# A cross-network kernel on one core: seven half-width matmuls in place of eight per 2x2 block of outputs

## The chip, the core and the metric

The kernel runs on one core of a Trainium2 chip. The metric is the device time of one launch in microseconds (us), the median of several runs. The core has a matrix engine (PE in the profile, PEld for its weight loads), a vector engine (DVE), a scalar engine (ACT), GpSimd (POOL) and a queue engine (SP) that issues most transfers. Matrix products accumulate in PSUM, which holds eight banks of 128 x 512 numbers; everything else lies in SBUF. All numbers are 32-bit floats.

## The reference

1024 rows, each with 64 features of 16 elements, go through three layers that multiply features pairwise; the rest is sums.

```
for i in range(3):                                   # W0, W1, W2
    z = einsum('bfe,bge->bfge', x0, h).reshape(B, f0 * fh, e)
    y = einsum('oc,bce->boe', W[i], z) + b[i][None, :, None]
    x_i, h = (y[:, :64], y[:, 64:]) if i < 2 else (y, y)
    xs.append(x_i)
pooled = sum(concatenate(xs, axis=1), axis=2)
return pooled @ fc_w.T + fc_b
```

## The kernel before

**What is computed.** The last layer is only ever summed with fixed weights, so the kernel folds W2, W1 and the final weights into one matrix at the start (the "set-up", up to some 46 us). After that each row needs two sets of 64 numbers, both linear in the products x_f * x_g of the row with itself: "h" (the kept half of layer one) and "q" (its partner). The result is the sum of (h + bias) * q, plus a small linear and quadratic part.

**Tiles.** The 1024 rows are 32 chunks of 32 rows, so a chunk is 512 columns (32 rows x 16 elements). The distinct products of a chunk are 16 tiles of 128 x 512; tile t = 4j + i. One `product` (line 234) makes the four tiles of one j: the operand `xa` (128 x 4 x 512) times the operand `xb` of that j (128 x 512). `contract` (line 256) sends the 16 tiles of a chunk through PE: 128 weight columns (64 of h, 64 of q, in `w_all`) against 512 columns, added up in one bank. Each such matmul stands as two rows in the trace, each with its weight load.

**Chunks.** Four chunks at the head (2, 3, 0, 1 in `HEAD`) get h alone first, by `half_contract` (line 297), because the q weights are not ready; q follows in `head_q` (line 315): 64 weight columns, one chunk in the upper and the other in the lower half of the array. The other 28 chunks go through `contract` whole. The squares and linear parts that the tiles leave over are `contract_shared` (lines 272, 277, 285): 24 matmuls of 32 rows x 64 columns for every four chunks.

**After PE.** For each chunk ACT copies the q half out of PSUM (line 331), DVE multiplies it with h (`factors`, line 337), and for each pair of chunks `x_v0x` (342) and `sums` (346) finish the row sums.

**Order.** The order is written out by hand: the list `order` and the loop behind it fix what each engine does next, and each engine works in that order, waiting for its inputs and for a free buffer. `load_products` loads a chunk's `xa` and `xb` on SP (1 MiB each) and has DVE make its 16 tiles; 12 buffers hold products, three each hold `xa` and `xb`. GpSimd makes only three groups of products, all at the head.

Of the kernel before, what the change touches and what calls it, by code (L numbers as in the profile page):

```python
# [42 lines left out]
F = 64  # L43
E = 16
# [15 lines left out]
FIRST = 4  # L60
SQ = slice(96, 128)


@with_exitstack
def cin_kernel(ctx, tc, xra, xrb, wh, w0r, w1h, w2t, wx1, wx0, vec, out):
# [3 lines left out]
    setup = ctx.enter_context(tc.tile_pool(name="setup", bufs=1))  # L69
    xp = ctx.enter_context(tc.tile_pool(name="xp", bufs=3))  # L70
    zp = ctx.enter_context(tc.tile_pool(name="zp", bufs=12))
# [8 lines left out]
    def z_tile(name):  # L80

        return zp.tile([128, NI, N], F32, tag="z", name=name)

    def flat_tile(name):
        return z_tile(name).rearrange("p i n -> p (i n)")

    def set_tile(name):
        return setup.tile([128, NI * N], F32, tag="set", name=name)
# [9 lines left out]
    nc.scalar.copy(fv2, fc2.to_broadcast([128, 32]))  # L98

    v0w = const_tile("v0w", [128, 2, F])  # L100
    v1w = const_tile("v1w", [128, 2, F])

    misc = ps.tile([128, N], F32, tag="acc", name="misc", bufs=4)

# [20 lines left out]
    w_all = const_tile("w_all", [128, NT, 192])  # L125
    w_sq = const_tile("w_sq", [128, 192])

    res = const_tile("res", [128, 128])


    xas, xbs, xxs, xrs, sqs = {}, {}, {}, {}, {}
# [12 lines left out]
    def load_xb(c, first=NJ):  # L144

        xb = xp.tile([128, NJ, N], F32, tag="xb", name=f"xb_{c}")
        for at in (slice(0, first), slice(first, NJ)):
            if at.start < NJ:
                nc.sync.dma_start(out=xb[:, at, :], in_=xrb[c, :, at, :])
        xbs[c] = [xb[:, j, :] for j in range(NJ)]  # L150

    def load_shared(first):

        xr = xrs[first] = sp.tile([128, 2, N], F32, tag="xr", name=f"xr_{first}")
        for k in (first // 2, first // 2 + 1):
            xxs[k] = sp.tile([128, N], F32, tag="xx", name=f"xx_{k}", bufs=4)
        for n in range(4):
            c = first + n
            nc.sync.dma_start(
                out=xr[32 * n : 32 * n + 32],  # L160
                in_=bass.AP(
                    tensor=xra.tensor, offset=c * XR * N, ap=[[N, 32], [32 * N, 2], [1, N]]
                ),
            )
            nc.sync.dma_start(out=xxs[c // 2][halves[c % 2]], in_=xra[c, 0:F])
        sqs[first] = sp.tile([128, N], F32, tag="sq", name=f"sq_{first}")
        nc.scalar.activation(sqs[first], xr[:, 0, :], AF.Square)  # L167
# [6 lines left out]
    w0t = z_tile("w0t")  # L174
    w2s = [flat_tile(f"w2_{k}") for k in range(2)]
    w1s = set_tile("w1s")
# [8 lines left out]
    xb_gps = xp.tile([128, NJ, N], F32, tag="xb", name="xb_gps")  # L185
# [4 lines left out]
    load_xb(c2, 1)  # L190
# [23 lines left out]

    acc = const_tile("acc", [128, 2, NCH // 2, CB])
    hb = const_tile("hb", [128, NF // 2, N])
    accs, uus, zs, ys, parts = {}, {}, {}, {}, {}
# [12 lines left out]
    def product(c, j, first=0, last=NI, engine=nc.vector):  # L230
        if first == 0:
            zs[c, j] = z_tile(f"z_{c}_{j}")
        at = slice(first, last)
        engine.tensor_tensor(  # L234
            zs[c, j][:, at, :], xas[c][:, at, :],
            xbs[c][j].unsqueeze(1).to_broadcast([128, last - first, N]), ALU.mult,
        )
        if j == NJ - 1:
            nc.scalar.activation(zs[c, j][SQ, 0, :], xas[c][SQ, 0, :], AF.Square)  # L239

    def w_cols(c):
        return slice(64, 192) if c % 2 else slice(0, 128)

    def tiles(j):

        return (1, 2, 3, 0) if j == NJ - 1 else range(NI)
# [5 lines left out]
    def contract(c, j, piece=0):  # L252
        acc_c, cols = pieces(c)[piece]
        for i in tiles(j):
            t = j * NI + i
            nc.tensor.matmul(  # L256
                acc_c, w_all[:, t, w_cols(c)], zs[c, j][:, i, cols],
                start=(t == 0 and c % 4 < 2), stop=(t == NT - NI and c % 4 >= 2),
            )

    def contract_shared(first):

        chunks = range(first, first + 4)
        ends = chunks if first == 0 else chunks[:2]
        for k in (first // 2, first // 2 + 1):
            ys[k] = ps.tile([128, N], F32, tag="y", name=f"y_{k}")
        groups = {c: slice(32 * (c % 4), 32 * (c % 4) + 32) for c in chunks}
        for m in range(2):
            for c, at in groups.items():
                n, xr = c % 2, xrs[first][groups[c], m]  # L270
                for acc_c, cols in pieces(c):
                    nc.tensor.matmul(  # L272
                        acc_c[halves[1 - n]], v1w[at, m], xr[:, cols],
                        start=(m == 0 and c not in ends), stop=False,
                        tile_position=(at.start, 64 * (1 - n)),
                    )
                nc.tensor.matmul(  # L277
                    ys[c // 2][halves[n]], v0w[at, m], xr, start=(m == 0), stop=(m == 1),
                    tile_position=(at.start, 64 * n),
                )  # L280
        for c, at in groups.items():
            for acc_c, cols in pieces(c):
                for n in range(2):
                    h = n == c % 2
                    nc.tensor.matmul(  # L285
                        acc_c[halves[n]], w_sq[at, w_cols(c)][:, 64 * n : 64 * n + 64],
                        sqs[first][at, cols], start=h and (first == 0 or c not in ends),
                        stop=(c in ends), tile_position=(at.start, 64 * n),
                    )


    def half_contract(c, *js, last=None):
        for j in js:
            for i in tiles(j):
                t = j * NI + i
                for n in range(2):
                    nc.tensor.matmul(  # L297
                        accs[c][halves[n]], w_all[:, t, 0:64],
                        zs[c, j][:, i, n * H2 : (n + 1) * H2],
                        start=(t == 0), stop=(j == last and i == tiles(j)[-1]),  # L300
                    )

# [8 lines left out]
    def head_q(k, j):  # L311
        for i in tiles(j):
            t = j * NI + i
            for c in (2 * k, 2 * k + 1):
                nc.tensor.matmul(  # L315
                    accs[c][halves[1 - c % 2]], w_all[:, t, 64:128], zs[c, j][:, i, :],
                    start=(t == 0), stop=False,
                )

    def uu_tile(k):  # L320
        if k not in uus:
            uus[k] = sp.tile([128, 2, N], F32, tag="uu", name=f"uu_{k}")
        return uus[k]

    def factors(c, which=slice(0, 1)):

        uu = uu_tile(c // 2)[halves[c % 2], 0, :]
        h = halves[c % 2]
        for acc_c, cols in pieces(c)[which]:
            q = sp.tile([128, N], F32, tag="q", name=f"q_{c}_{cols.start}")  # L330
            nc.scalar.copy(q[h, cols], acc_c[64 - h.start : 128 - h.start])  # L331
            if c in HEAD:
                hc = hb[h, c // 2, :]
                nc.vector.tensor_tensor(hc, acc_c[h], hc, ALU.add)
                nc.vector.tensor_tensor(uu, hc, q[h], ALU.mult)
                continue
            nc.vector.scalar_tensor_tensor(  # L337
                uu[:, cols], acc_c[h], bh1[h], q[h, cols], ALU.add, ALU.mult
            )

    def x_v0x(k):
        nc.vector.scalar_tensor_tensor(uu_tile(k)[:, 1, :], ys[k], cx, xxs[k], ALU.add, ALU.mult)  # L342

    def sums(k, rows=slice(0, 128), of=slice(0, 2), half=slice(0, CB)):
# [3 lines left out]
            uus[k][rows, of, E * half.start : E * half.stop].rearrange("p k (b e) -> p k b e", e=E),  # L348
# [17 lines left out]
    nc.scalar.copy(xb_gps[:, 0, :], xbs[c0][1])  # L366
    xbs[c0][1] = xb_gps[:, 0, :]
# [11 lines left out]
    nc.vector.memset(w0o[3][SQ, 0, :], 0.0)  # L379
    for j in (2, 3):  # L380
        h1_weights(j, w0o[j])
    half_contract(c0, 0)
# [8 lines left out]
    nc.scalar.copy(xb_gps[:, 1, :], xbs[c1][3])  # L391
    xbs[c1][3] = xb_gps[:, 1, :]
# [12 lines left out]
    v2r = flat_tile("v2r")[:, 0:1024].rearrange("p (n c) -> p n c", n=2)  # L405
    v2t = res[:, 0:F]
    for n in range(2):
# [7 lines left out]
        nc.vector.transpose(v2r[:, n, :], pv)  # L415


    v2q = v2r.rearrange("p n (s r) -> p (n s) r", r=32)[:, :, 0]
    for h in range(2):
        at = slice(32 * h, 32 * h + 32)  # L420
        nc.vector.tensor_copy(v2t[halves[h], at], v2q[halves[h]])
        nc.scalar.copy(v2t[halves[1 - h], at], v2q[halves[h]])
    half_contract(c1, 0, 3, 1)


    m_sb = z_tile("m_sb")
# [4 lines left out]
    for m in (0, 1):  # L431
        for n in range(2):
            for h in range(2):
# [3 lines left out]
                )  # L437

# [32 lines left out]
    )  # L471

# [4 lines left out]
    nc.scalar.copy(cx, pcx)  # L477
# [4 lines left out]
    for j in range(NJ):  # L482
        product(c2, j)
    product(c3, NJ - 1, engine=nc.gpsimd)
# [3 lines left out]
    ms = set_tile("ms").rearrange("p (v t g) -> p v t g", v=2, g=F)  # L488
# [30 lines left out]
    for j in range(NJ - 1):  # L519
        product(c3, j)  # L520
# [6 lines left out]
    dg = res[:, F:128]  # L527
    nc.sync.dma_start(out=dg[SQ], in_=m_ap(32, 32, [[row + F, 32], [1, F]]))
    nc.sync.dma_start(out=w_sq[:, 64:128], in_=m_ap(0, 0, [[0, 4], [row + F, 32], [1, F]]))
# [7 lines left out]

# [258 lines left out]
```

## Time and profile before

| | |
|---|---|
| time of three runs | 484.93, 485.12, 485.13 us; median 485.12 us |
| span of the profiled execution | 483.0 us, 4429 instructions |
| around the span, against the median | 2.1 us |
| line 256 (128 weight columns), PE | 387.6 us busy, 928 rows |
| line 315 (64 weight columns), PE | 27.9 us busy, 128 rows |
| line 234, DVE | 278.3 us busy, 124 groups of four tiles, 2285 ns each |
| transfers | 87.01 MB, mean 180 GB/s |
| clock of PE | 1.000 of full speed throughout |

The page prints the span of the one profiled execution and not its time; its own time is taken as the span and the 2.1 us around it. In the rows, "out<-in" names the tile written and the tiles read, then partitions x elements; "x64" counts rows; a bracket at the end tells how long the engine stood idle before and what ended that. Busy times of neighbouring instructions overlap by their ends, so the distance between two starts is the better price of an instruction in a row of equals.

### The profile page before, as it was taken

To read this page: it belongs to the slowest core of one execution; us is meant where nothing else is said; L and a number is where in the kernel's file an instruction comes from. 1 tells how busy PE (TensorE), PEld (TensorE's weight loads), DVE (VectorE), ACT (ScalarE), POOL (GpSimd) and SP (SyncE) were. 2 spreads that over 40 slices of the span, in tenths; PEclk is the share of its full clock that TensorE was granted. 3 is DMA by queue.
4 is the path that set the end of the run, shared out by engine and by line. 5 is a ranking of instruction groups with operands and counts; after the bars stand their busy time and mean duration, and the time that the engine had idled before them with its cause. 6 is when DMAs were issued, how large, how long until landed. Compare 5 with 4: busy or idle time off the path is not lost.

```text
span 483.0 us, 4429 instructions
## 1 busy us (share of the span) xinstructions
PE 478.9 (99%) x1808; PEld 215.6 (45%) x1808; DVE 368.6 (76%) x227; ACT 67.5 (14%) x143; POOL 15.4 (3%) x17
## 2 busy tenths in 40 slices
PE   8999999999999999999999999999999999999997
PEld 4564344443344444444444444444444444444555
DVE  4993699998899988898887686766878677771321
ACT  3242033011110111001100010001000010000001
POOL 5330000000000000000000000000000000000000
PEclk9999999999999999999999999999999999999999
DMA  8986997662962683487247344373346631000000
GB/s 328 415 271 178 386 364 296 216 219 101 341 241 102 221 280 120 176 280 279 110 169 210 159 174 175 151 214 105 139 174 210 224 125 51 0 1 0 0 1 1
DMA packets 19660, 87.01 MB, mean 180 GB/s; under 512 B 4820, under 2 KB 5492, under 8 KB 10744
## 3 DMA queue, kind: packets, MB, share of 16 engines
q1 hardware_dynamic: 18584, 85.71, 49.8%
q10 hardware_dynamic: 1056, 1.02, 0.9%
q8 instruction: 14, 0.23, 0.2%
q14 instruction: 6, 0.05, 0.0%
HBM read 85.08 MB, written 1.64 MB: 180 GB/s over the span
## 4 chain that ended last, share of the span: by engine, by line
PE 98%; DMA 1%; DVE 1%; issue 0%; ACT 0%
PE acc L256 80%; PE acc L315 6%; PE acc L297 6%; PE acc L272 3%; PE acc L285 1%; PE xp L204 1%; DMA xa<-in_xra 1%; DVE z L234 1%; PE pm L434 0%; PE pv L410 0%; PE y L277 0%; PE pl L715 0%; DVE uu L337 0%; PE pc L651 0%; PE po L612 0%
## 5 line engine op out<-in xcount | busy, mean ns | idle before, releaser
L256 PE MATMUL acc<-z,w_all 128*128 128x512 f32 (+2 forms) x928 | 387.6, 579 | 0.0
L234 DVE TENSOR_TENSOR z<-xa,xb 128x2048 f32<-128x2048 f32 x124 | 278.3, 2285 | 41.4 <-PE acc L256 35.1
L256 PEld LDWEIGHTS acc<-z,w_all 128*128 128x128 f32 x928 | 173.1, 190 | 213.0 <-issue 205.9
L239 ACT ACTIVATE z<-xa 32x512 f32<-32x512 f32 x34 | 21.3, 626 | 336.9 <-DVE z L234 334.9
L337 DVE SCALAR_TENSOR_TENSOR uu<-acc,vs,q 64x512 f32<-64x512 f32 (+2 forms) x29 | 21.2, 731 | 58.0 <-ACT q L331 57.8
L297 PE MATMUL acc<-z,w_all 128*64 128x256 f32 x256 | 28.9, 381 | 0.4 <-DVE z L234 0.4
L315 PE MATMUL acc<-z,w_all 128*64 128x512 f32 x128 | 27.9, 593 | 0.0
L331 ACT COPY q<-acc 64x512 f32<-64x512 f32 (+2 forms) x33 | 18.7, 566 | 35.9 <-PE acc L256 19.8
L297 PEld LDWEIGHTS acc<-z,w_all 128*64 128x64 f32 x256 | 17.8, 137 | 12.7 <-DVE z L234 2.0
L234 DVE TENSOR_TENSOR z<-xa,xp 128x2048 f32<-128x2048 f32 (+2 forms) x12 | 20.3, 1747 | 0.7 <-PE xp L204 0.7
L346 DVE TENSOR_REDUCE acc<-uu 128x64 f32<-128x1024 f32 (+3 forms) x18 | 20.0, 1117 | 0.3
L315 PEld LDWEIGHTS acc<-z,w_all 128*64 128x64 f32 x128 | 9.1, 137 | 18.0 <-issue 16.8
L277 PE MATMUL y<-xr,v0w 32*64 32x512 f32 x128 | 15.9, 600 | 0.0
L272 PE MATMUL acc<-xr,v1w 32*64 32x512 f32 (+2 forms) x132 | 15.7, 587 | 0.0
L342 DVE SCALAR_TENSOR_TENSOR uu<-y,cx,xx 128x512 f32<-128x512 f32 x16 | 11.3, 747 | 0.2
L272 PEld LDWEIGHTS acc<-xr,v1w 32*64 32x64 f32 x132 | 5.1, 131 | 10.0 <-issue 9.0
L234 POOL TENSOR_TENSOR z<-xa,xb_gps 128x512 f32<-128x512 f32 (+2 forms) x4 | 9.4, 2373 | 4.8 <-ACT xb_gps L366 4.8
L285 PE MATMUL acc<-sq,w_sq 32*64 32x512 f32 (+2 forms) x132 | 8.7, 574 | 0.0
L533 DVE TENSOR_TENSOR w_all<-ms 128x256 f32<-128x256 f32 x4 | 1.5, 424 | 5.4 <-DMA ms<-md 5.4
L167 ACT ACTIVATE sq<-xr 128x512 f32<-128x512 f32 x8 | 5.0, 630 | 3.3 <-DMA xr<-in_xra 3.1
L204 PE MATMUL xp<-xa,shift 64*64 64x512 f32 x32 | 5.2, 754 | 0.3 <-DMA xa<-in_xra 0.3
L285 PEld LDWEIGHTS acc<-sq,w_sq 32*64 32x64 f32 x132 | 3.7, 132 | 3.7 <-issue 3.5
(66 smaller groups left out, 69.5 us busy)
## 6 DMA issues: line engine op xcount, KB each, us to landing
xa<-in_xra SPq DMA_DIRECT2D x32, 1024.0 KB
xb<-in_xrb SPq DMA_DIRECT2D x31, 1024.0 KB, 7.1
xr<-in_xra SPq DMA_DIRECT2D x32, 128.0 KB, 13.7
xx<-in_xra SPq DMA_DIRECT2D x32, 128.0 KB, 7.7
w<-in_w2t SPq DMA_DIRECT2D x2, 1024.0 KB, 12.0
w1s<-in_w1h SPq DMA_DIRECT2D x1, 1024.0 KB
w1x<-in_wx SPq DMA_DIRECT2D x1, 1024.0 KB
w0x<-in_wx SPq DMA_DIRECT2D x1, 1024.0 KB, 6.0
```

The costliest lines, as they stand in the source:

```text
L234: engine.tensor_tensor(zs[c, j][:, at, :], xas[c][:, at, :], xbs[c][j].unsqueeze(1).to_broadcast([128, last - first, N]), ALU.mult,)
L239: nc.scalar.activation(zs[c, j][SQ, 0, :], xas[c][SQ, 0, :], AF.Square)
L256: nc.tensor.matmul(acc_c, w_all[:, t, w_cols(c)], zs[c, j][:, i, cols], start=(t == 0 and c % 4 < 2), stop=(t == NT - NI and c % 4 >= 2),)
L272: nc.tensor.matmul(acc_c[halves[1 - n]], v1w[at, m], xr[:, cols], start=(m == 0 and c not in ends), stop=False, tile_position=(at.start, 6 ...
L277: nc.tensor.matmul(ys[c // 2][halves[n]], v0w[at, m], xr, start=(m == 0), stop=(m == 1), tile_position=(at.start, 64 * n),)
L285: nc.tensor.matmul(acc_c[halves[n]], w_sq[at, w_cols(c)][:, 64 * n : 64 * n + 64], sqs[first][at, cols], start=h and (first == 0 or c not ...
L297: nc.tensor.matmul(accs[c][halves[n]], w_all[:, t, 0:64], zs[c, j][:, i, n * H2 : (n + 1) * H2], start=(t == 0), stop=(j == last and i == ...
L315: nc.tensor.matmul(accs[c][halves[1 - c % 2]], w_all[:, t, 64:128], zs[c, j][:, i, :], start=(t == 0), stop=False,)
L331: nc.scalar.copy(q[h, cols], acc_c[64 - h.start : 128 - h.start])
L337: nc.vector.scalar_tensor_tensor(uu[:, cols], acc_c[h], bh1[h], q[h, cols], ALU.add, ALU.mult)
L342: nc.vector.scalar_tensor_tensor(uu_tile(k)[:, 1, :], ys[k], cx, xxs[k], ALU.add, ALU.mult)
L346: nc.vector.tensor_reduce(acc[rows, of, k, half], uus[k][rows, of, E * half.start : E * half.stop].rearrange("p k (b e) -> p k b e", e=E), ...
```

## The change

**Seven for eight.** Chunks are taken two at a time, b and a, and tiles t and t + 8 (j and j + 2) together. A 2x2 block of outputs (h and q, of b and a) over two tiles is eight matmuls of 64 weight columns. The change uses a scheme with seven, whose operands are sums and differences of tiles and of weights. It applies to 7 of the 8 tile pairs (`GROUPS`) of 12 of the 16 chunk pairs (k = 3 to 14). Chunks 4, 5, 30, 31 keep plain contraction, and the head's 0 to 3 stay as they were.

**Where the operands come from.** The weight sums (`ws`) are made once. Of the four sums of tiles, one comes from adding two `xb` operands before the product (`w_both` on DVE, then `w_product` into "T3"); the other three are differences of finished tiles, made by GpSimd (`w_mix`, 128 x 2048 and 128 x 1536 alternating, six per chunk pair). Every `xb` operand of a DVE product is first copied by ACT into a PSUM bank (`second`); the two banks of tag "y" serve for that.

**Results.** The seven products go into three accumulators, `alpha`, `delta`, `beta`, each 64 rows of a bank, one array half or the other. Partial values are copied out on the way by ACT (`snap_p1`, `snap_p7`, `snap_u2`); DVE puts them together (`w_hb`, `w_qa`, `w_ha`, `w_uu`). A pair's last products and its results fall into the next pair's window (`first_fill`, `second_fill`, `late_run`, `end_pair`).

**Leftovers.** `contract_shared` goes; six matmuls of 64 weight columns per pair take its place (`q_extra` with 128 rows, `h_extra` and `v0x` with 64), reading a new operand `e` (256 KiB a chunk).

**Order.** All work behind the head is entered in a list with a time in units of one matmul (`at(when, ...)`) and issued in that order; a window is `SPAN` = 31 units. PE alternates between the array halves. 14 buffers (`take`, `used`) hold tiles; `xb` is loaded by quarters of 256 KiB (nine buffers). The folding of the linear weights (`weigh`) moves to GpSimd, and so do four more groups of plain products, of chunks 5, 2 and 3.

```diff
+    def second(c, j):
+        bank = ps.tile([128, N], F32, tag="y", name=f"xp_{c}_{j}")
+        nc.scalar.copy(bank, xbs[c][j])
+        xbs[c][j] = bank
...
+    def w_run(p, out, w, name, start=False, at_t=0):
+        return [
+            (w_job, p, out, w, j * NI + i + at_t, name, start and n == 0)
+            for n, (j, i) in enumerate(GROUPS)
+        ]
...
+    def w_product(p, c, j, name, uses):
+        p.setdefault(name, {})[j % 2] = b = take(uses)
+        nc.vector.tensor_tensor(
+            blocks[b], xas[c], xbs[c][j].unsqueeze(1).to_broadcast([128, NI, N]), ALU.mult
+        )
+
+    def w_both(p, j):
+        bank = xbs[p["b"]][j + 2]
+        nc.vector.tensor_tensor(bank, bank, xbs[p["b"]][j], ALU.add)
+        xbs[p["b"]][j] = bank
...
+        tiles = slice(j, NI)
+        nc.gpsimd.tensor_tensor(
+            blocks[o][:, tiles], blocks[x][:, tiles], blocks[y][:, tiles], ALU.subtract
+        )
...
+    def snap_u2(p):
+        nc.scalar.activation(snaps[1][p["O"]], alpha(p), AF.Identity, bias=bh1[p["A"]])
...
+        for when, c, j, name, uses in (
+            (-21.4, b, 2, "B22", 5), (-15.8, a, 0, "X", 5), (-12.2, b, 3, "B22", 6),
+            (-2, a, 1, "X", 6), (1.6, a, 2, "B21", 5), (4.2, a, 3, "B21", 6),
+        ):
+            at(t + when - 2.7, second, c, j)
+            at(t + when, w_product, p, c, j, name, uses)
+        for j, (d, t3) in enumerate(((-18.7, -18.4), (-9.5, -6.1))):
+            at(t + d, w_both, p, j)
+            at(t + t3, w_product, p, b, j, "T3", 9)
+        for when, j, *names in (
+            (-7, 0, "T2", "T3", "X"), (0.7, 1, "T2", "T3", "X"),
+            (4.7, 0, "T3", "B22", "T2"), (10, 1, "T3", "B22", "T2"),
+            (15.2, 0, "T2", "T2", "B21"), (20.5, 1, "T2", "T2", "B21"),
+        ):
+            at(t + when, w_mix, p, j, *names)
...
+            w_run(p, alpha, wq_all, "X", True) + fill[0] + w_run(p, alpha, s2, "T2")
+            + fill[1] + w_run(p, alpha, s1, "T3")
+            + [
+                (w_job, p, alpha, wh_all, NI, "T3"), (w_job, p, alpha, s1, NI, "B22"),
+                (lambda: h_extra(b, p["alpha"]),), (v0x, b, "set"),
+            ],
+            w_run(p, delta, s3, "T3", True) + late
+            + w_run(p, beta, wq_all, "B21", True, 2 * NI) + w_run(p, delta, neg, "T2"),
+        )
+        at(t + 6.8, snap_p1, p)
+        at(t + 6.9, snap_p7, p)
+        at(t + 6.8 + len(fill[0]) + 7, snap_u2, p)
...
+    for j in range(NJ - 1):
+        plain_product(14.8 + 2.6 * j, 2, j)
...
+    zipped(32, *extras(2, "y"))
...
+    T0 = 52
...
+    def constant():
+        pc = ps.tile([128, 1], F32, tag="y", name="pc")
...
+    at(15.5, constant)
```

## The prediction

> **What bounds the kernel now.** First the page: the shares of the engines and the chain that ended last.
>
> ```profile
> PE 478.9 (99%) x1808; PEld 215.6 (45%) x1808; DVE 368.6 (76%) x227; ACT 67.5 (14%) x143; POOL 15.4 (3%) x17
> ...
> PE 98%; DMA 1%; DVE 1%; issue 0%; ACT 0%
> ```
>
> PE is never idle and alone on the path, so a matmul less is worth its full time, as long as the engines that feed PE keep up. Then the timeline of PE, for the price of a matmul:
>
> ```profile
> 42.00 13.90 PE L315 MATMUL acc<-z,w_all 128*64 128x512 f32 x64
> 55.84 27.73 PE L256 MATMUL acc<-z,w_all 128*128 128x512 f32 x64
> 83.50 0.64 PE L272 MATMUL acc<-xr,v1w 32*64 32x512 f32 x1
> 83.51 0.64 PE L277 MATMUL y<-xr,v0w 32*64 32x512 f32 x1
> ...
> 85.27 1.06 PE L285 MATMUL acc<-sq,w_sq 32*64 32x512 f32 x16
> 86.26 24.30 PE L256 MATMUL acc<-z,w_all 128*128 128x512 f32 x56
> ```
>
> Line 256: 32 full-width matmuls (64 rows) from 55.84 to 83.50, 0.864 us each. Line 315: 32 matmuls of 64 columns from 42.00 to 55.84, 0.865 us for each two, so two half matmuls run side by side. I call 0.865 us a slot. The leftovers take 83.50 to 86.26, 2.76 us per four chunks. Last, the timelines of DVE, GpSimd and SP, for the work that the change adds:
>
> ```profile
> 29.89 6.68 DVE L234 TENSOR_TENSOR z<-xa,xp 128x2048 f32<-128x2048 f32 x3
> ...
> 78.63 26.50 DVE L234 TENSOR_TENSOR z<-xa,xb 128x2048 f32<-128x2048 f32 x12
> 105.05 1.52 DVE L337 SCALAR_TENSOR_TENSOR uu<-acc,vs,q 64x512 f32<-64x512 f32 x2
> 106.61 1.41 DVE L342 SCALAR_TENSOR_TENSOR uu<-y,cx,xx 128x512 f32<-128x512 f32 x2
> 107.93 1.21 DVE L346 TENSOR_REDUCE acc<-uu 128x64 f32<-128x1024 f32 x1
> ```
>
> ```profile
> 30.21 4.57 POOL L234 TENSOR_TENSOR z<-xa,xb 128x2048 f32<-128x2048 f32 x1 [13.78 <-DMA xb<-in_xrb]
> ```
>
> ```profile
> 44.42 0.40 SPq L136 DMA_DIRECT2D xa<-in_xra  x1
> ```
>
> A DVE product costs 26.50/12 = 2.21 us in a row; with a PSUM operand (xp) also 2.2, while GpSimd works beside it at 4.57.
>
> **PE after.** Until 42.00 nothing on PE changes. In a window one array half gets 32 matmuls, of which two couples (64 rows each, upper and lower, as the 32-row matmuls above run together) share a slot; the other gets 31. That is 31 slots, 26.8 us, where a pair took 32 x 0.864 + 2.76/2 = 29.0. From 42.00: 16 slots (q of 0, 1), 32 (chunks 4, 5), 2 (leftovers), 16 (q of 2, 3), 28 (first window, which has the head's leftovers as filling), 11 x 31, 12 + 2 (the last pair's results) and 16 (chunk 30): 465 slots, 402.2 us, to 444.2. In the old timeline of ACT the q copy behind chunk 30 starts at 465.1, so chunk 31 and the end take 483.0 - 465.1 = 17.9. Sum: a span of 462.1 if PE never waits, 20.9 less than 483.0. The weight sums cost nothing on the path: four GpSimd operations of 128x512 (1.28 us) and a copy on ACT, beside the 13.8 us of PE from 42.00 on; first used at 107. The squares that ACT no longer writes into tiles (line 239, 34 x 0.63) lay in ACT's idle time.
>
> **What must keep up in a window of 26.8 us.** DVE: 8 products x 2.21 = 17.7; two sums of operands 2 x 0.68 (128x512 rows); three 64x512 with a scalar 3 x 0.75 (749 ns by form), two without 2 x 0.69 (686 ns); x_v0x 0.75 and sums 1.2: 24.6. GpSimd: 3 x 4.57 and 3 x 3.47 (128x1536, midway between the rows of 2374 and 4559 ns): 24.1. ACT: 8 copies and 3 partial values x 0.59, 2 squares x 0.63: 7.8. Transfers: 4.75 MiB. In the stretch 46 to 58 us the trace moved about 410 GB/s, 2.56 us per MiB: 12.2 us. All fit, DVE with 2.2 us to spare. I followed one window in issue order: DVE waits for ACT's copy behind `snap_p1` (7.6 us into the window), has its last product for the next window, X of j = 1, ready 26.9 us in, and PE asks for it four slots into the next, at 30.3. GpSimd waits for PE to finish reading T2 (slot 15, 13.0 us), delivers the new T2 at 17.7 and 21.2; asked for at 20.8 and 24.2. So PE keeps 3 us of cover on each, and a window costs its 26.8.
>
> **The start is where it does not fit.** SP's first load of chunk 4 was issued at 44.42 and goes to some 43.5 (one small load fewer ahead of it). Data came 1.3 us after the issue and the last byte is seen 0.8 later; then 2.56 us per MiB. Ahead of the second loading of chunk 2 stand 8 MiB (chunks 4 and 5, four `e`, two weight arrays, `xa` of 2) and four `xx` of 64 rows that move at about 215 GB/s (2.5 us): its first `xb` lands at 69.3, its last at 71.3. DVE is through with chunk 5 at 65.0 and waits; ACT copies (0.6); the product of chunk 2 runs 70.0 to 72.2.
> - PE reaches `constant` at 69.7. Its bank is one of the two "y" banks, held by that product: wait of 2.6 us, to 72.3. Chunk 5 ends at 86.1.
> - GpSimd's line is chunk 5 (58.5, as it lands), first weights (to 67.7), chunk 2 (71.3 to 75.9), second weights (80.5). DVE then adds up (82.8), two products of chunk 3 (87.2), and for pair 3 B22, the sum and T3: 92.4. `v0x` of chunks 4, 5 takes the "y" bank that holds this shared operand, so PE, there at 87.0, waits 5.5 us. Q of 2, 3 ends at 107.2.
> - In the first window DVE waits for `y` and makes the head's results (2 x 4.6 us) among its products. T3 of the next pair ends at 122.8; with only one "y" bank free, copy and product alternate: X 125.7, copy 126.4, and only then ACT's queue reaches `snap_u2` (127.0), which PE needs at slot 18, 122.8. Wait of 4.3 us. The next window starts at 135.8, and X of j = 1 (138.5) is in time for 139.2.
>
> Together 12.4 us. What of this the nearest rows leave open: from 0 (the loads land 5 us earlier and DVE runs ahead) to 20 (they share the queue as at 60 to 64 us, 247 GB/s). I take 12.4, because its rows are of the same queue and the same engines. At the end, chunk 31 as half matmuls of 128 columns doubles the instructions: 0 to 1.5 us, taken as 0.5 (by the 256-column rows of line 297, 0.44 us a couple against half of 0.865). New to the trace is GpSimd's subtract beside a busy DVE: at best DVE's 2.21 for the shape (then nothing changes, PE is the bound), at worst GpSimd and DVE take turns, 24.1 + 24.6 us a window, which the row at 30.21 excludes. Nearest is that row, 4.57.
>
> Span 462.1 + 12.4 + 0.5 = 475.0; with one of the 50 ns semaphore rows of line 234 open in each of 11 windows, 475.6. The 2.1 us around the span stay: **477.7 us**, against 485.1 (median) or 483.0 + 2.1 (profiled).
>
> **Two rules weighed.** Rows: the 32 half matmuls of line 315 keep a slot of 0.865 although each has its own two weight loads (137 ns each in PEld), both halves using all 128 rows. The Trainium skill, "TensorE: Matmul & The Clock Gate", Part 3, "The mechanism", says a weight load overlaps with running matmuls only when its row group differs. By that, four loads of 137 ns would stand open in every slot, 0.55 us, and this kernel would lose over 200 us; the rows above deny it. Rows: at 30.21 GpSimd's two-input product and three DVE products with one PSUM operand ran beside each other at their usual 4.57 and 2.21. "GPSIMD Engine Reference", section 1, names a shared SBUF interface with contention where DVE has two SBUF inputs. `second` avoids that for products; the head's four h x q (two SBUF inputs) would meet it, by that page up to four GpSimd operations of 4.57 us (an estimate), and no row here shows it.
>
> **Rivals.**
> - *The start is covered.* Loads and GpSimd are ahead, PE waits under 6 us. For: PE waited 0.4 us in all of the old start. Against: DVE stood 6.0 us waiting for `xb` at 46 to 52, on the same queue. 464 to 471, say 467.
> - *Small waits in every window* (0.3 to 0.6 us, ACT's single queue between copies and `snap_u2`): 11 x 0.45 = 5 on top: 483.
> - *GpSimd becomes the bound.* Its six subtracts follow each other through DVE's X and PE's T2. At more than 26.8/24.1 x 4.57 = 5.1 us each (128x2048) it sets the window; the gain is gone at windows of 27.5 (477.7 + 11 x 0.67 = 485.1), that is at 5.2 us, and from there the kernel is slower than before. At 5.5 us the windows take 29.0: 502. For: the trace never has GpSimd, DVE, ACT and transfers busy together for long. Against: the one row beside DVE is undisturbed.
> - *The halves don't run together* with different weights and data in each. Against: lines 272 and 277 start 0.01 us apart with different weights. One weight load open per slot (0.14): 11 x 31 x 0.14 = 48: 526.
>
> **Chances.** Forecast (471 to 482) 0.50; covered start (464 to 471) 0.18; small waits 0.10 (of it 0.02 within 0.2% of before); GpSimd or DVE the bound 0.18 (0.16 slower, half of it below 488; 0.02 the same); halves apart 0.04. About 0.2%, 1 us, is what a measurement can tell from no change. Faster 0.76, same 0.04, slower 0.20. The range 464 to 488 leaves out 0.12 to 0.15; the faster cases alone have 464 to 484.
>
> **What would show it.** A half matmul couple of 0.865 us and starts of windows 26.8 us apart; idle PE at some 70 (2.6 us, behind DVE), 87 (5.5) and 123 us (4.3, behind ACT), and hardly any after 140; GpSimd's subtract at 4.57 and 3.47. The forecast is wrong if GpSimd rows exceed 5 us, if DVE products beside them pass 2.4, or if PE is idle once in every window.

## The result, and the profile after

The change makes the kernel slower: 540.61 us (median of four runs, 534.98 to 541.56) against 485.02 us; the ratio is 1.1125 (95% interval 1.1074 to 1.1176). The profiled execution took 541.56 us, with a span of 539.8 us: 64.2 us above the forecast span of 475.6. First the page again: busy shares, the clock in forty slices, and the chain that ended last.

```profile
PE 521.8 (97%) x2308; PEld 175.6 (33%) x2308; DVE 402.6 (75%) x280; ACT 114.0 (21%) x210; POOL 335.3 (62%) x100
...
PEclk9999979999799999999999999999999999999999
...
PE 81%; DMA 7%; DVE 5%; POOL 3%; SPq 2%; issue 1%; ACT 1%; DVEq 0%; POOLq 0%
```

PE is still nearly always busy and most of the chain. So the time is not lost in waiting for the new engines. The groups by shape say the same of the new work on GpSimd and DVE (count, busy us, mean ns, then idle time and what ended it):

```profile
L663 POOL TENSOR_TENSOR z<-z,z 128x2048 f32<-128x2048 f32 x36 | 164.4, 4566 | 65.9 <-PE delta L538 41.1 <-PE alpha L538 15.3 <-DVE z L647 9.5
L663 POOL TENSOR_TENSOR z<-z,z 128x1536 f32<-128x1536 f32 x36 | 124.8, 3467 | 36.6 <-DVE z L647 36.6
...
L647 DVE TENSOR_TENSOR z<-xa,xp 128x2048 f32<-128x2048 f32 x96 | 217.8, 2282 | 47.7 <-PE delta L538 26.0 <-ACT xp L566 20.4 <-POOL z L663 0.4
```

The durations are the forecast ones, and both feeders wait for PE, GpSimd for 56 us in all (41.1 + 15.3). PE is busy but slow: from one window to the next the same matmul (`beta<-e,va`) starts at 252.42, 408.36 (five windows) and 439.55, so a window takes 31.19 us, where 26.8 was forecast. A stretch of PE's timeline in the middle of a window (start us, us, then the instruction; each matmul is two rows, "x2" groups them) shows why:

```profile
228.10 0.59 PE L538 MATMUL delta<-z,w_all 128*64 128x512 f32 x1
228.10 0.59 PE L538 MATMUL beta<-z,w_all 128*64 128x512 f32 x1
228.53 0.59 PE L538 MATMUL delta<-z,w_all 128*64 128x512 f32 x1
228.53 0.59 PE L538 MATMUL beta<-z,w_all 128*64 128x512 f32 x1
229.06 1.07 PE L538 MATMUL delta<-e,vs 64*64 64x512 f32 x2
230.06 1.07 PE L538 MATMUL beta<-z,w_all 128*64 128x512 f32 x2
231.06 1.07 PE L538 MATMUL y<-e,v 64*64 64x512 f32 x2
232.06 0.64 PE L538 MATMUL beta<-z,w_all 128*64 128x512 f32 x1
232.06 0.64 PE L538 MATMUL alpha<-z,ws 128*64 128x512 f32 x1
```

Read the starts. Two half matmuls of 128 rows stand side by side (228.10, 228.53: a couple takes 0.86 us). Then a leftover of 64 rows (`h_extra`) runs alone for 1.00 us, the 128-row matmul of the other half behind it runs alone for 1.00 us, and the next leftover (`v0x`) alone again; only then do couples return. At the end of the window there are four more such lone steps (a `delta` at 239.83, `h_extra` at 240.78, a `delta` at 241.78, `v0x` at 242.79). So 63 half matmuls are 28 couples and 7 lone ones: 28 x 0.857 + 7 x 1.0 = 31.0, against 31.19 measured.

The three waits of PE that were forecast are there, of other sizes (us in total, times, longest):

```profile
PE alpha L538 <- ACT snap L674: 6.6, 1, 6.6
PE pc L873 <- DVE z L239: 5.5, 1, 5.5
PE y L538 <- DVE z L647: 1.2, 1, 1.2
```

Behind the two long ones PE worked at half its clock. The table by stretches has the granted clock ("PEclk") third from the right: 0.50 and 0.75 behind the wait that ended at 76.3, 0.50 behind the one that ended at 139.4.

```profile
76.00:80.00 4.00, 3.71 (x12) 1.84 (x14) 4.00 (x3) 1.86 (x7) 4.00 (x1) 0.50 1.06 398
80.00:84.00 4.00, 4.00 (x18) 1.20 (x16) 2.83 (x2) 0.59 (x1) 4.00 (x2) 0.75 0.89 321
...
139.30:143.30 4.00, 3.94 (x10) 1.38 (x12) 3.94 (x5) 2.86 (x5) 3.19 (x1) 0.50 0.00 0
```

**Where the 64 us are**, by starts in PE's timeline:

| stretch | forecast | measured | more |
|---|---|---|---|
| up to the first window | to 107.2 | to 111.43 | 4.2 |
| first window | 24.2 + 4.3 wait | 150.22 - 111.43 = 38.8 | 10.3 |
| eleven windows | 26.85 each | 31.19 each | 47.7 |
| from 493.3 to the end | 12.1 + 13.8 + 18.4 = 44.3 | 539.8 - 493.3 = 46.5 | 2.2 |

### The profile page after: what moved, and what is told of

It is laid out like the page before. It is cut to its first block, busy times and chain, and to the rows that moved or that the text cites. A ratio compares the mean times of both kernels' runs of the same rounds, so it can differ in the third digit from the quotient of the medians.

```text
span 539.8 us, 6085 instructions
## 1 busy us (share of the span) xinstructions
PE 521.8 (97%) x2308; PEld 175.6 (33%) x2308; DVE 402.6 (75%) x280; ACT 114.0 (21%) x210; POOL 335.3 (62%) x100
## 3 DMA queue, kind: packets, MB, share of 16 engines
q10 hardware_dynamic: 1056, 1.02, 0.7%
## 4 chain that ended last, share of the span: by engine, by line
PE 81%; DMA 7%; DVE 5%; POOL 3%; SPq 2%; issue 1%; ACT 1%; DVEq 0%; POOLq 0%
PE alpha L538 31%; PE delta L538 19%; PE beta L538 15%; PE acc L538 6%; PE y L538 4%; DMA z<-in_wx 3%; PE acc L271 3%; DVE z L647 2%; PE acc L253 2%; POOL z L239 2%; DMA e<-in_xra 1%; DVE uu L288 1%; DMA md<-z 1%; DMA xb<-in_xrb 1%; DMA z<-md 1%
## 5 line engine op out<-in xcount | busy, mean ns | idle before, releaser
L663 POOL TENSOR_TENSOR z<-z,z 128x2048 f32<-128x2048 f32 x72 | 287.2, 4017 | 102.5 <-DVE z L647 46.1
L647 DVE TENSOR_TENSOR z<-xa,xp 128x2048 f32<-128x2048 f32 x96 | 217.8, 2282 | 47.7 <-PE delta L538 26.0
L538 PE MATMUL alpha<-z,ws 128*64 128x512 f32 x576 | 209.5, 597 | 6.6 <-ACT snap L674 6.6
L538 PE MATMUL delta<-z,ws 128*64 128x512 f32 x336 | 153.1, 602 | 0.0
L538 PE MATMUL beta<-z,w_all 128*64 128x512 f32 x216 | 103.8, 598 | 0.0
L566 ACT COPY xp<-xb 128x512 f32<-128x512 f32 x92 | 53.6, 588 | 209.7 <-DVE z L647 178.4
L538 PE MATMUL alpha<-z,w_all 128*64 128x512 f32 x192 | 86.9, 595 | 0.0
L538 PEld LDWEIGHTS alpha<-z,ws 128*64 128x64 f32 x576 | 63.3, 138 | 64.8 <-issue 64.3
L239 DVE TENSOR_TENSOR z<-xa,xp 128x2048 f32<-128x2048 f32 (+2 forms) x32 | 65.1, 2080 | 13.2 <-ACT xp L566 10.6
L538 PE MATMUL acc<-z,w_all 128*128 128x512 f32 (+3 forms) x256 | 58.5, 508 | 0.0
L538 PE MATMUL delta<-z,w_all 128*64 128x512 f32 x48 | 24.5, 592 | 0.0
```

What stands on the lines that cost most here:

```text
L239: engine.tensor_tensor(blocks[zs[c, j]][:, at, :], xas[c][:, at, :], xbs[c][j].unsqueeze(1).to_broadcast([128, last - first, N]), ALU.mult,)
L538: nc.tensor.matmul(out, w, rhs, start=start, stop=stop, skip_group_check=True)
L566: nc.scalar.copy(bank, xbs[c][j])
L647: nc.vector.tensor_tensor(blocks[b], xas[c], xbs[c][j].unsqueeze(1).to_broadcast([128, NI, N]), ALU.mult)
L663: nc.gpsimd.tensor_tensor(blocks[o][:, tiles], blocks[x][:, tiles], blocks[y][:, tiles], ALU.subtract)
```

## The experiments

**The theory** after the result: matmuls over different numbers of rows don't stand side by side on PE. At each change between 64 and 128 rows PE runs dry, and a leftover in the stream of 128-row couples can cost a neighbour as well as itself. The Trainium skill has such a rule, which the prediction overlooked: "TensorEngine Tiling (Array Packing)", Tiling Modes, Key Properties, says that changing the tiling mode, and not just the tile, drains TensorE; 128 and 64 rows are different modes there. It gives no price. **Rivals**: the leftovers run alone because of their place in the queue, or because of a wait for operand or bank; or each costs 1 us by itself wherever it stands; or the feeders set the window.

**Padding (e1_pad).** Same matmuls, same order, but 128 rows: the missing rows of weights are zeros.

```diff
+    w0z = const_tile("w0z", [128, F])      # rows 0 to 63 zero, 64 to 127 as w0ds
...
-            mm(acc_c[halves[c % 2]], w0ds[halves[1]], es[c][halves[1], cols], start=start)
+            mm(acc_c[halves[c % 2]], w0z, es[c][:, cols], start=start)
...
-        mm(ys[c // 2][halves[c % 2]], v0[halves[0]], es[c][halves[0]], start=True, stop=True)
+        mm(ys[c // 2][halves[c % 2]], v0, es[c], start=True, stop=True)
```

> The leftovers h_extra and v0x get weights of 128 rows, half of them zeros, in place of 64 rows; the number of matmuls and their order stay. Theory (a matmul over 64 rows can't stand beside one over 128 rows, so PE changes over before and after it and both halves' neighbours run alone): all 63 half matmuls of a window now alternate between the array halves, 31.5 couples of 0.856 us = 27.0 us from window to window in place of 31.2, 46 us less in eleven windows and 3 to 5 less in the first window and at the end: 488 to 493 us. Rival A (the leftovers run alone for another reason: two in a row in one array half, or a wait for their operand or bank): windows stay at 31.2, 540 us. Rival B (PE gets faster, but DVE at 24.6 or GpSimd at 24.1 us a window, or ACT's queue, holds it): windows of 27.5 to 29 with idle PE in each, 495 to 515 us.

Measured 497.62 us (497.36 to 498.53), ratio to the kernel before 1.0237 (1.0216 to 1.0259): 43 us less than the change. Ten windows take 428.90 - 158.53 = 270.37 us, 27.04 each, as the theory says to 0.04 us; both rivals fall. The same place of the window in PE's timeline of this kernel:

```profile
220.27 0.59 PE L542 MATMUL beta<-z,w_all 128*64 128x512 f32 x1
220.33 0.59 PE L542 MATMUL delta<-e,w0z 128*64 128x512 f32 x1
...
221.13 0.59 PE L542 MATMUL beta<-z,w_all 128*64 128x512 f32 x1
221.19 0.59 PE L542 MATMUL y<-e,v 128*64 128x512 f32 x1
```

Each leftover now has a partner that starts 0.06 us apart. The total is 5 us above the expected 488 to 493. Most of that lies at the start: the waits there take 15.5 us in place of 13.3 (8.6 us at `snap_u2`, 4.9 at `constant`, 2.0 at `y`), and a slow clock now stands behind each of them. Behind the one at `y` the head's second q takes 15.60 us in place of 13.95.

**Side by side (e2_side).** The 64 rows stay; only the order differs.

```diff
-            (lambda: h_extra(a, p["delta"]),), (v0x, a, "set"),
+            (lambda: (h_extra(a, p["delta"]), v0x(a, "set")),),
...
-                (lambda: h_extra(b, p["alpha"]),), (v0x, b, "set"),
+                (lambda: (h_extra(b, p["alpha"]), v0x(b, "set")),),
```

> The leftovers keep their 64 rows, but the h_extra and v0x of a chunk (upper and lower rows) are issued next to each other, with no matmul of the other half between. Theory (change-over between row counts): 7 lone matmuls a window become 2 couples of 64 rows at 1.0 us and 3 lone ones of 128 rows, because one array half has 31 matmuls of 128 rows and the other 28: 28 x 0.856 + 3 x 0.86 + 2 x 1.0 = 28.6 us a window, or 27.3 if the three find partners: 540.6 less 11 x 2.6 to 3.9 = 498 to 512 us. Rival A (each leftover matmul pays 1.0 us for itself wherever it stands): 4 x 1.0 + 59 x 0.43 and the lone ones = 30 to 31.2 us a window, 528 to 540 us.

Measured 514.47 us (510.69 to 516.01), ratio 1.0569 (1.0520 to 1.0618). A window takes (417.23 - 157.05)/9 = 28.91 us, 0.3 above the theory's 28.6 and 1.1 to 2.3 below rival A's 30 to 31.2; the total is 2.5 us above the theory's 498 to 512. The two leftovers share one step, upper and lower rows:

```profile
222.69 0.64 PE L538 MATMUL delta<-e,vs 64*64 64x512 f32 x1
222.69 0.64 PE L538 MATMUL y<-e,v 64*64 64x512 f32 x1
...
223.69 0.64 PE L538 MATMUL beta<-z,w_all 128*64 128x512 f32 x1
```

From 222.69 to 223.69 is 1.00 us for both, what one took alone. So two matmuls with the same row count do run side by side; what costs is going from one row count to the other.

**Half of it padded (e9_half).** As e1_pad, but `v0x` keeps its 64 rows.

> The change with h_extra padded to 128 rows and v0x left at 64: two changes of the row count and back in a window in place of four. Theory: two lone matmuls at 1.0 us and 61 half matmuls in couples of 0.857: 28.1 us a window, 509 us; 29.1 and 520 if each change-over also leaves a neighbour alone. Rival (the cost is one of padding or of the h_extra alone): 27.0 or 31.2.

One run: 517.44 us; a window takes (420.31 - 160.20)/9 = 28.90 us. That is nearer the dearer version. Each `v0x` runs alone for 1.00 us. At the first one of a window (226.68) the neighbours stay in couples; at the second a `delta` runs alone for 0.95 us as well:

```profile
226.68 1.07 PE L542 MATMUL y<-e,v 64*64 64x512 f32 x2
...
236.32 1.02 PE L542 MATMUL delta<-z,ws 128*64 128x512 f32 x2
237.27 1.07 PE L542 MATMUL y<-e,v 64*64 64x512 f32 x2
238.27 0.64 PE L542 MATMUL alpha<-z,w_all 128*64 128x512 f32 x1
```

Windows of 27.04, 28.90 and 31.19 us with none, two and four leftovers of 64 rows: 0.93 us for each of the first two, 1.04 on the mean of four. e2_side has four leftovers of 64 rows, but in two groups, and its window of 28.91 us is that of e9_half with two. So the time goes with the number of changes to 64 rows and back, not with the number of 64-row matmuls.

**The head's products (e3_hq).** The rest of the loss lies at the start. In the head's results DVE multiplies h by q, both from SBUF (line 288):

```profile
122.92 2.71 DVE L288 TENSOR_TENSOR uu<-hb,snap 64x512 f32<-64x512 f32 x1
...
126.38 4.18 DVE L288 TENSOR_TENSOR uu<-hb,snap 64x512 f32<-64x512 f32 x1
...
142.18 0.86 DVE L288 TENSOR_TENSOR uu<-hb,snap 64x512 f32<-64x512 f32 x1
...
143.80 0.69 DVE L288 TENSOR_TENSOR uu<-hb,snap 64x512 f32<-64x512 f32 x1
```

At 143.80 GpSimd was idle. Beside the other three it worked, and each of them ended 0.5 to 0.6 us behind a subtract on GpSimd: at 125.63 (GpSimd at 125.08), 130.56 (130.02) and 143.04 (142.49). The subtract had started first each time, and the one from 125.49 took the usual 4.53 us.

```diff
-                nc.vector.tensor_tensor(hc, acc_c[h], hc, ALU.add)
-                nc.vector.tensor_tensor(uu[h, 0, :], hc, q, ALU.mult)
+                nc.vector.tensor_tensor(acc_c[h], acc_c[h], hc, ALU.add)
+                nc.vector.tensor_tensor(uu[h, 0, :], acc_c[h], q, ALU.mult)
```

> The four products h x q of the head's chunks (lines 287 and 288) read h from PSUM in place of SBUF; the sum before them is written to PSUM. Theory (a DVE operation with both inputs in SBUF waits while GpSimd works): the rows of 2.71 and 4.18 us fall to 0.7, DVE reaches the next pair's products 5.5 us earlier, ACT's copies and with them snap_u2 too, PE's wait of 6.6 us falls to 0 to 2 and its slow clock behind it (2 us) goes: 531 to 535 us. Rival A (the rows are long for another reason): rows and time unchanged, 540. Rival B (rows shrink, but another feeder holds PE at the same place): rows of 0.7, wait still above 4 us, 537 to 540.

Measured 536.31 us (535.01 to 536.50), ratio 1.1020 (1.0992 to 1.1049), 4.3 us less than the median of the change (one of whose four runs took 534.98). The long rows are gone; the last line is GpSimd's in the same run:

```profile
125.36 0.68 DVE L288 TENSOR_TENSOR uu<-acc,snap 64x512 f32<-64x512 f32 x1
...
139.14 0.68 DVE L288 TENSOR_TENSOR uu<-acc,snap 64x512 f32<-64x512 f32 x1
127.92 12.46 POOL L663 TENSOR_TENSOR z<-z,z 128x2048 f32<-128x2048 f32 x3 [2.26 <-PE alpha L538]
```

The product at 139.14 lies wholly beside a subtract and takes 0.68 us; so do two in e7_gp (119.28 and 120.74, 0.68 and 0.69 us, GpSimd busy from 109.29 to 128.55). That shows the contention. The two products that had been long fell, in this run, mostly into a gap of GpSimd (125.65 to 127.92), so how much of the 4.3 us is due to the operand and how much to that shift is not shown. PE's wait at `snap_u2` fell from 6.6 to 1.1 us. The time is 1.3 us above the 531 to 535 expected; this execution lost 1.1 us more at `constant` (6.6) and 1.7 at the head's second q, which ran at a slow clock (15.65 us for line 271 against 13.95).

**The order at the start (e4_start, e5_start).** Both kernels have the padding and e3's products, and `constant` stands ahead of the head's first q, where banks are free. In e4_start `snap_u2` of the first pair simply stands earlier, so there it reads the partial value before all of T2's matmuls are in it, which changes what that pair computes; its time stands for the order alone. In e5_start the copies and products of the second pair's operands go behind `snap_u2` instead. (The remarks behind # in this cut and the next are the document's.)

```diff
-    at(15.5, constant)
+    constant()                       # ahead of head_q_tile(0, ...)
...
-        at(t + 6.8 + len(fill[0]) + 7, snap_u2, p)                    # e4 alone
+        at(t + (12 if p["k"] == 3 else 13.8 + len(fill[0])), snap_u2, p)
...
+            if p["k"] == 4 and -16 < when < -12:                      # e5
+                u, v = t - 14 + (when + 16) / 10, max(v, t - 13.3)
```

> Padded leftovers, h read from PSUM in the head's products, and two moves: the two small matmuls of constant go ahead of the head's q, and in the first window ACT takes snap_u2 ahead of two copies of operands. Theory: beside the windows of 27.0 us the waits of 5.5 us (constant) and 6.6 us (snap_u2) go with the slow clock behind each (2.5 and 2 us), 490 - 16 = 474 us; since DVE and the transfers are late at the start anyway (DVE idle 9 us at 66 to 74 us for loads), half of it may come back as PE waits for the operands of pair 3 or for the bank of y: 472 to 484. Rival (the start is set by the loads and DVE, and PE's waits only move): 485 to 490, as the padded leftovers alone.

> Padded leftovers, h of the head from PSUM, constant ahead of the head's q as in the kernel before, and in the first window ACT's two copies of the next pair's operands stand behind snap_u2, with their products behind them, so that snap_u2 reads the finished partial value. Theory (PE's waits at the start are queue order, and each costs again by a slow clock behind it): windows of 27.0 us, no wait above 4 us, 488 to 492 us; loads and DVE hold the rest, because DVE has 77 us of work between the arrival of chunk 2 and the second window. Rival (the copies were needed early): DVE's products come later, PE waits as long at the second window, 496 to 500.

Measured 490.65 us (490.32 to 491.41; ratio 1.0093, 1.0072 to 1.0113) and 490.95 us (490.39 to 492.16; ratio 1.0119, 1.0092 to 1.0147). The first expectation was 7 to 19 us too low, and its rival (485 to 490, the waits only move) came nearest: the gain over e1_pad is 7 us. The second was right in time (488 to 492), but for one wait above its 4 us. The waits went from where they were repaired and came back behind: in e5_start PE waits 4.1 us for the bank of `y`, 3.7 us for squares of `e` on ACT, whose queue stood behind a copy that waited for GpSimd's weights, and 2.9 us at the second window.

**Loads (e6_loads) and work for GpSimd (e7_gp).** Next, 2.5 MiB of loads go behind the second loading of chunk 2, squares ahead of the waiting copy, two reductions of weights behind products, and in e7_gp two groups of products go to GpSimd as well.

```diff
-    for n in (4, 5, 0, 1):
-        load_e(n)
...
-    at(-2, load_wx, 0, wx0)
+    at(4.1, load_wx, 0, wx0)
+    for n in (4, 5):
+        at(4.2, load_e, n)
...
+            if p["k"] == 3 and name == "B21":                         # e7
+                at(t - 6 + j, w_product, p, c, j, name, uses, nc.gpsimd)
```

> As the kernel with the moved copies, and on SP the second weight array, the four e and the xx (2.5 MiB) go behind the second loading of chunk 2; squares go ahead of a copy that waits for GpSimd, the two reductions of weights behind products. Theory (DVE is the bound from some 66 to 148 us, and its 6 us of idle time for chunk 2 is on the path): chunk 2 lands 4 to 6 us earlier, PE reaches the second window as much earlier, 483 to 487 us. Rival (chunk 2 waits for free buffers of xb, not for the queue): its landing and the time stay, 489 to 492.

> As the kernel with the moved loads, and GpSimd makes two groups of products of the first pair (B21) in its idle stretch, in place of DVE: 9.1 us of GpSimd for 4.6 us of DVE. Theory (DVE the bound of the start): another 3 to 4.5 us, 479 to 484 us. Rival (GpSimd's next subtracts come later and hold PE in the first window): no gain or up to 3 us more, 484 to 490.

Measured 485.71 us (483.64 to 486.15; ratio 0.9995, 0.9982 to 1.0009) and 485.16 us (483.98 to 487.06; ratio 0.9992, 0.9976 to 1.0009). These moves together were worth 5 us, as expected (483 to 487); the products on GpSimd, from which 3 to 4.5 us were expected, nothing that can be told. DVE's timeline in e7_gp shows where most of the 4.6 us that were freed went:

```profile
104.67 4.49 DVE L660 TENSOR_TENSOR z<-xa,xp 128x2048 f32<-128x2048 f32 x2
115.70 2.29 DVE L660 TENSOR_TENSOR z<-xa,xp 128x2048 f32<-128x2048 f32 x1 [6.55 <-ACT xp L579]
```

DVE was through earlier and then idle, 6.55 us in place of the 3.26 before the same product in e6_loads: its next operand is a copy on ACT that stands in ACT's queue behind `snap_p1`, which waits for PE. Work of DVE was not the bound there, order was.

**Three moves (e8_order).** The `v0x` of chunks 4 and 5 go behind the head's second q; the loads and squares of `e` for chunks 2 and 3 go back, so that ACT's copies don't stand behind them; the second pair's first operands are made ahead of `snap_p1` and the head's results.

```diff
-    zipped(32, *extras(2, "y"))
+    zipped(32, *(column[:2] for column in lists))
+    zipped(51, *(column[2:] for column in lists))
...
-        at(34.9, load_e, n)
-        at(36, square, n)
+        at(51.2, load_e, n)
+        at(56, square, n)
...
+            if p["k"] == 4 and j == 2 and name == "B22":
+                u = t - 24.35
...
+            if p["k"] == 4 and j == 0:
+                d, t3 = -20.2, -20.1
```

> As the kernel with two groups of products on GpSimd, and three moves at the start: the v0x of chunks 4 and 5 go behind the head's second q (so PE doesn't wait 4.5 us there for a bank of y), the loads of e of 2 and 3 and their squares go back (ACT's copies wait behind them, DVE stood 4.5 us for that), and the first operands of the second pair are made ahead of the head's results (DVE stood 6.6 us behind a copy that stood behind snap_p1). Theory (the rest of the start is queue order too): 5 to 9 us less than 485.2: 476 to 480. Rival (DVE's work between chunk 2 and the second window is the bound, whatever the order): PE waits in the first window instead, 482 to 486.

Measured 477.89 us (476.85 to 479.00), ratio 0.9827 (0.9805 to 0.9848), inside the 476 to 480 expected: less than both kernels, 1.7% less than the one before. What PE still waits for beyond the set-up (waits of 1 us and more):

```profile
PE delta L551 <- POOL z L676: 2.6, 1, 2.6
...
PE alpha L551 <- DVE snap L694: 1.2, 1, 1.2
```

**Both halves of the loss apart (e10_rows64).** e8_order with the leftovers back at 64 rows.

> The kernel with the three moves at the start, but h_extra and v0x back at their 64 rows, as in the change itself. Theory (the change-over of row counts costs 4.15 us in each of eleven windows and some 1 to 2 us in the first window and at the end, whatever the start is like): 477.9 + 45.7 + 1 to 2 = 524 to 526 us. Rival (padding gained partly because it moved PE against DVE and GpSimd at the start, so the two repairs overlap): under 520 us.

Measured 524.46 us (523.41 to 524.98), ratio 1.0783 (1.0748 to 1.0819), inside the 524 to 526; a window takes (422.94 - 142.24)/9 = 31.19 us. So the two repairs add up to within 3.6 us: with the old start, padding is worth 540.6 - 497.6 = 43.0 us; with the new start, 524.5 - 477.9 = 46.6 us. The new start is worth 16.1 us (540.6 - 524.5) without padding and 19.7 (497.6 - 477.9) with it.

## Why the prediction was wrong

- **PE is the bound**: right. 97% busy; GpSimd and DVE wait for it.
- **Prices of the feeders**: right. GpSimd 4.57 and 3.47 us, a DVE product 2.28. In each of the windows between 154 and 341 us DVE was busy 24.5 to 24.7 us (24.6 forecast), GpSimd 23.9 to 24.6 (24.1).
- **The step that failed**: "In a window one array half gets 32 matmuls, of which two couples (64 rows each, upper and lower, as the 32-row matmuls above run together) share a slot ... That is 31 slots, 26.8 us." The rows it was read from are 32-row matmuls beside 32-row ones. In the change's order each 64-row matmul follows a 128-row one and stands before another. The change between row counts, which the sum had at nothing, is the term that was missing: the runs put 4.15 us a window in place of nothing (31.19 against 27.04 with equal rows), 45.7 us in eleven windows. With equal rows the 31.5 couples cost 27.04 us, 0.2 above the forecast.
- **The start** (12.4 us of waits): the three places were right, the sizes not: 5.5 us at `constant` (2.6 forecast), 1.2 at `y` (5.5), 6.6 at `snap_u2` (4.3), 13.3 in all. Missed was the slow clock behind the long ones, some 2 us each (four passes of 0.85 us in place of 0.43 behind 139.36; chunk 5 in 16.3 us in place of 13.8).
- **The clock** as the Trainium skill has it: "TensorE: Matmul & The Clock Gate", Part 1, says that an idle window of about 3.4 us puts TensorE back to half rate for about as long. The waits of 5.5 and 6.6 us agree. After shorter ones the rows go both ways: 1.25 us (the change) left the head's second q at 13.95 us, while 1.50 (e3_hq) and 1.99 (e1_pad) were followed by 15.65 and 15.60, with a clock of 0.50 to 0.57 on the way. So the page's figure does not tell by itself which of these short waits is followed by a slow clock.
- **The two rules that the prediction weighed**: "GPSIMD Engine Reference", section 1, is borne out: the head's four products took 8.4 us in place of 4 x 0.69 = 2.8, and one took 0.68 beside GpSimd with one input in PSUM (139.14 in e3_hq). The sum had put this at nothing. The other, on weight loads in the mechanism part, stays denied as the prediction read it: couples of 128 rows run at 0.857 us, and each half matmul has two loads of its own. The same part also lets a load go ahead into a background weight buffer, which the prediction left out and which these rows would fit.
- **The rivals**: none happened. "GpSimd becomes the bound" fell by its own sign (no row above 5 us), "small waits in every window" too (three long waits, none in the windows). "The halves don't run together" is the nearest in time (526), but by another mechanism: they do run together with different weights, and not with different row counts. The case that came true was not among them.

What stays open: why a lone 64-row matmul takes 1.00 us where half a couple would take 0.43 and 128-row matmuls in a row in one half 0.87 (3.48 us for four, from 501.59). An open weight load of 0.13 us would fit the difference, and no run here separates it from the running dry. That PE runs dry is the page's explanation; the runs show the price of the change and that equal row counts remove it, not what happens inside.

## What to carry to other kernels

"These two run side by side" has to be read from rows in which the same two shapes stand next to each other in the same order; rows of like beside like say nothing about mixtures. Before small matmuls are used as filling among large ones, give them the same number of rows, with zero weights if need be: a zero row costs nothing, a change to 64 rows and back cost about 1 us here. And an operand queue that stands still for one late copy (ACT behind `snap_p1`, squares behind a reduction) is worth checking before work is moved to another engine: reordering (e8_order) gave 7 us after offloading (e7_gp) had given none.

## What was not expected of the hardware

- A 64-row matmul of 512 columns between 128-row ones takes 1.00 us alone and often leaves a neighbour alone for 0.95 to 1.00 us; four 64-row ones in four quadrants together took 1.02 us as well (118.40 to 119.42 in the change).
- A DVE instruction with both inputs in SBUF took 2.71 and 4.18 us in place of 0.69 while GpSimd worked. GpSimd's instruction beside it, which had started first, kept its 4.53 us; no row has DVE starting first. With one input in PSUM DVE's took 0.68 us beside GpSimd.
- A wait of PE of only 1.5 to 2.6 us was followed by a slow clock in three kernels (e3_hq, e1_pad, and e8_order, with 0.50 behind the wait of 2.6), and one of 2.9 us (second window of e5_start) by none: 1.00 behind it.
